# Block 0's left and right sides evicted whole, its context put inside block 1, block 1's rows turned by VectorE

## The chip, the cores and the metric

The kernel runs on one core of a Trainium2 chip. The metric is the time of one execution on the device, in microseconds. A core has five engines that run side by side and wait for one another by semaphores: TensorE (PE; its weight loads are listed as PEld), VectorE (DVE), ScalarE (ACT), GpSimd (POOL) and SyncE (SP), which here only issues DMAs. DMAs are issued from the queues of SyncE, ScalarE and GpSimd. Each engine works through its own instructions in program order, so an instruction that waits holds up all that stand behind it on its engine.

## The reference

Everything is float32. `x` is [128, 64, 768]: 128 graphs of 64 nodes, `adj` is [128, 64, 64]. Two layers, each followed by a residual and a layer norm.

```
layer 0, per graph:
u    = x x^T / sqrt(768);  p = softmax(u);  delta = p * adj
attn = delta / (sum(delta) + 1e-10)
ctx  = upper(attn) (x W_left^T + b_left) + diag(attn) * (x W_self^T + b_self)
       + lower(attn) (x W_right^T + b_right)
x    = layernorm(x + relu(layernorm(ctx) * gamma + beta))
layer 1, per graph, 12 heads of 64:
q, k, v = x Wq + bq, x Wk + bk, x Wv + bv
s    = q k^T / 8 + beta1 * adj, masked where adj <= 0
x    = layernorm(x + softmax(s) v)
```

## The kernel before, in words

The 8192 rows are cut into 16 blocks of 512 rows: four tiles `t` of 128 rows, each holding two graphs (`g`). Layer 0 of block `n+1` is interleaved with layer 1 of block `n`. The last loop (`for n in range(NBLK)`) is that steady part; ahead of it stands a hand-written start, the part that the change edits: layer 0 of block 0, then layer 0 of block 1, while all six weight matrices are turned into the forms that the steady loop reads.

**Products with fewer multiplications.** A product of 512 rows with a 768x768 matrix is done in seven smaller ones (`seven`, `by_tokens`), in the order 1, 2, 6, 5, 7, 4, 3. Each of the seven is done for two halves `j` of the tokens, three matmuls of 128x384 each (the profile counts each float32 matmul as two). The partial sums sit in two PSUM tags, `ps_X` (1, 6, 7, 4) and `ps_Y` (2, 5, 3), with two buffers each. After a group VectorE evicts it: after 1, 6 and 7 into a temporary `u` (line 575, adding a bias), after 2, 7, 4 and 3 into the result (`last`). A group that goes on adding to a bank must wait until the bank's eviction is done, so a late VectorE stops TensorE. A group of 12 takes TensorE 3.87 us. Between groups `step()` takes one waiting piece of other work off a queue (`first`, `urgent`, `lazy`): sums of weights, softmax, norms.

**Weights.** `prepare` loads a matrix in quarters (`b_s`, `b_l`, `b_r`), VectorE forms differences (`t_s`, `t_l`, `t_r`; lines 352 and 354), and the results are stored to DRAM (`d_s`, `d_l`, `d_r`) for block 1. `prepare1` does Wv, Wq and Wk: nine raw pieces are loaded from ScalarE's queue (line 268) into *homes*, VectorE forms fifteen sums, and GpSimd's queue stores them (`v_d`, line 275; `qk_d`, lines 282 and 284). A home is used again when its store has landed. For Wv there are 16 homes (six slices of a transposed-row tile `xT`, four of the later outputs `x1`, six of the pool `prep`), for Wq and Wk 11 of the pool `prep1`, which lies where `prep` was.

**Rows.** A block's rows must be transposed before they can be multiplied. Blocks 0 and 1 are transposed by TensorE (`transposed`, line 397), with ScalarE copying the result out of PSUM (line 398). From block 2 on the rows are loaded in 32x32 order (`squares`, line 407) and VectorE turns them (`turned`, line 416, six instructions of 128x512 per block). The rows of block 1 are loaded by SyncE into `rows` (line 1216).

**Attention and context.** `attention0` runs the scores `u` (line 703), then the softmax, and GpSimd forms the sums of rows (`combined`). `sides` transposes the attention weights (`ps_a`, line 754). `context0` multiplies them with the left and right results, 8 matmuls of 64x384 for two tiles (`ps_ctx`, line 879), and VectorE adds the diagonal part (line 887). Its last part starts the norm: statistics, square root (ScalarE, line 518), scale (910, 914), residual (917), a second norm (924, 928), after which `transposed1(0)` turns block 0 for layer 1.

**The layout that the context needs.** For the context the left result of the second graph has to lie in the upper 64 partitions beside the right result. Block 0 does it in the eviction: two instructions on 64 partitions each (line 807). Blocks 1 and on evict 128 partitions in one (line 801), and ScalarE swaps the two half-tiles later through a spare tile (`swapped`, lines 786 to 788: three copies of 64x768 per tile).

**Order in the start.** Scores of block 0; self of block 0 (weights `b_s`, `t_s`); left of block 0 (`b_l`, `t_l`), while `b_r` is prepared; `sides(0)`; right of block 0, while Wv is prepared; all of block 0's context; rows of block 1 transposed; scores of block 1; then self, left and right of block 1 (`ws`, `wl`, `wr`), while Wq and Wk are prepared; `transposed1(0)`; then the steady loop. The Tile scheduler orders each engine's instructions by the priority of their place in the program and by its estimate of times; `tc.issue_after(x)` forbids a place ahead of `x`. SyncE's queue holds, in order: `xa` (block 0's rows), `b_s`, `bs`, two `adj`, `rows`, `b_l`, the left and right biases, gamma, beta, `bv`, a third `adj`, `b_r`, `bq` and `bk` in columns (line 103), `abeta`, and then `ws`.

Of the kernel before, what the change touches and what calls it, by code (L numbers as in the profile page):

```python
# [17 lines left out]
P = 128  # L18
# [52 lines left out]
def gnn_two_layers(ctx: ExitStack, tc, x, adj, wl, bl, ws, bs, wr, br, gamma, beta,  # L71
# [29 lines left out]
    def column(v, name):  # L101
        t = const.tile([P, KC], F32, tag=name, name=name)
        nc.sync.dma_start(out=t, in_=v.rearrange("(c p) -> p c", p=P))  # L103
        return t
# [6 lines left out]
    abeta_c = const.tile([P, 1], F32, tag="abeta", name="abeta")  # L111

# [123 lines left out]
    def homes_of_v():  # L236

        xT = tp.tile([P, KC, NTOK], F32, tag="xT", name="h_v")
        yield from (xT[:, c, :] for c in range(KC))
        for t in range(T):  # L240
            yield x1_p.tile([P, D], F32, tag="x1", name="h_v")[:, 0 : 2 * TH]

    def prepare1(nm, homes, queue=lazy):
# [16 lines left out]
        def loaded(i):  # L260
# [6 lines left out]
            with tc.issue_after(recent["exp"].ins) if nm == "v" else ExitStack():  # L267
                nc.scalar.dma_start(out=raw, in_=w[:, 2 * k : 2 * k + 2, j * TH : (j + 1) * TH])
# [416 lines left out]
    def attention0(n, sums=True):  # L685
# [13 lines left out]
        for t in range(T):  # L699
            for c in range(KC):  # L700
                for g in range(2):
                    tok = slice(t * P + g * L, t * P + (g + 1) * L)
                    nc.tensor.matmul(u[g * L : (g + 1) * L, t, :], lhsT=xT[:, c, tok], rhs=xT[:, c, tok],  # L703
                                     start=(c == 0), stop=(c == KC - 1))
# [77 lines left out]

    def swapped(lr, t):
# [4 lines left out]
        nc.scalar.copy(low, swap[0:L, 0:D])  # L788

    def side_part(n, nm, in_sbuf, hooks={}):  # L790
# [7 lines left out]
        def last(t, h, ps, part):  # L798
            cols = slice(h * HALF, (h + 1) * HALF)
            if n > 0:  # L800
                recent["u"] = nc.vector.tensor_tensor(lr[t][:, "lr".index(nm), cols], ps,
                                                      bias[nm][:, cols] if part is None else part, ALU.add)
                return
            for g in range(2):
                rows = slice(g * L, (g + 1) * L)
                half = "lr".index(nm)
                recent["u"] = nc.vector.tensor_tensor(lr[t][half * L : (half + 1) * L, g, cols], ps[rows],
                                                       bias[nm][rows, cols] if part is None else part[rows], ALU.add)
# [48 lines left out]
    def context0(n):  # L857
# [13 lines left out]
        banks = {}  # L871
# [10 lines left out]
        def part(t):  # L882
# [8 lines left out]
            elif t == T - 1:  # L891
# [305 lines left out]

    def now(fs):
# [9 lines left out]
    edges(0)  # L1208
    attention0(0)
# [4 lines left out]
    rows = sq_p.tile([P, T, D], F32, tag="sq", name="rows")  # L1214
    for t in range(T):
        nc.sync.dma_start(out=rows[:, t, :], in_=x_t[1, t])
    blocks[1]["rows"] = [rows[:, t, :] for t in range(T)]
# [333 lines left out]
```

## Time and profile before

| | us |
|---|---|
| median of three runs | 2799.73 |
| lowest and highest | 2798.21, 2800.53 |
| the profiled execution | 2799.42 |
| its span | 2797.7 |

The span is the stretch that the trace covers; 1.7 us of the execution lie around it. In the page each group of instructions has its line, engine, operation, output, input, count, busy time, mean duration and the idle time of the engine just before it with what ended it. In a timeline a row is a start, a length, the engine, the line and the operation, and in square brackets the idle time before it. The mean granted TensorE clock of the core is given as 0.999.

### The profile page before, as it was taken

What the parts mean: (1) busy time and instruction counts of PE and PEld (TensorE: products, weight loads), DVE (VectorE), ACT (ScalarE), POOL (GpSimd) and SP (SyncE); (2) the same over time, 40 slices, a digit from 0 to 9 for tenths busy, and PEclk for the clock granted to TensorE, in tenths of its full rate; (3) what the DMA queues carried; (4) which work ended last, traced back from release to release, by engine and by line L of the source; (5) the groups of instructions that cost most, each with busy time, mean ns of one, the idle gap of its engine ahead of it and who ended that gap; (6) DMA issues with size and microseconds to landing.
All of it is one profiled execution on the core that took longest, in us unless ns stands there. A gap on an engine that the chain in (4) does not pass through costs nothing.

```text
span 2797.7 us, 49397 instructions
## 1 busy us (share of the span) xinstructions
PE 2775.1 (99%) x17962; PEld 2013.5 (72%) x17962; DVE 1934.7 (69%) x3380; ACT 1115.1 (40%) x1916; POOL 962.6 (34%) x1251
## 2 busy tenths in 40 slices
PE   8999999999999999999999999999999999999998
PEld 5558677686776867768587685867768677686787
DVE  5767668676675766767677676776767668676667
ACT  0014344335343452434525344353433534345244
POOL 3243334415144141432415225061351513415122
PEclk9999999999999999999999999999999999999999
DMA  9687787958769486695866858578585876948543
GB/s 339 199 299 248 216 256 242 264 151 250 208 186 275 142 267 189 196 266 151 268 180 211 249 170 269 159 229 233 182 259 157 249 208 183 279 143 260 177 129 110
DMA packets 394848, 604.88 MB, mean 216 GB/s; under 512 B 49296, under 2 KB 277648, under 8 KB 394608
## 3 DMA queue, kind: packets, MB, share of 16 engines
q1 hardware_dynamic: 338992, 495.73, 59.3%
q0 software_dynamic: 18704, 76.89, 7.6%
q10 hardware_dynamic: 36912, 29.10, 5.1%
q8 instruction: 146, 2.39, 0.4%
q14 instruction: 94, 0.77, 0.1%
HBM read 530.00 MB, written 78.45 MB: 217 GB/s over the span
## 4 chain that ended last, share of the span: by engine, by line
PE 94%; DVE 2%; DMA 2%; issue 1%; SPq 0%; ACT 0%; POOL 0%; POOLq 0%; DVEq 0%; ACTq 0%
PE ps_X L480 26%; PE ps_Y L480 17%; PE ps_Y L836 13%; PE ps_X L836 11%; PE ps_X L542 10%; PE ps_Y L542 8%; PE ps_ctx L879 3%; PE sc L1041 2%; PE u L703 2%; PE ps_y L1104 2%; PE ps_X L588 1%; DMA qk_d<-h_qk 1%; SPq L103 0%; PE ps_x L397 0%; DMA h_qk<-in_L_gnn_Wk_dram 0%
## 5 line engine op out<-in xcount | busy, mean ns | idle before, releaser
L428 POOL TENSOR_TENSOR sums<-hT 128x768 f32<-128x768 f32 x16 | 29.0, 1811 | 790.3 <-PE ps_X L480 775.5
L1074 ACT ACTIVATE eT<-s 32x384 f32<-32x384 f32 x512 | 266.6, 521 | 33.6 <-PE ps_y L1104 17.0
L480 PE MATMUL ps_X<-xT,wqk 128*128 128x256 f32 x1024 | 234.2, 379 | 0.2 <-ACT xT L398 0.2
L890 ACT ACTIVATE unused<-o 128x768 f32<-128x768 f32 x60 | 50.6, 843 | 440.5 <-DMA sq<-in_x_dram 224.4
L610 DVE TENSOR_TENSOR lr<-ps_Y,u_deep 128x384 f32<-128x384 f32 x273 | 151.7, 556 | 95.3 <-PE ps_Y L836 78.8
L1017 ACT ACTIVATE qk<-ps_X,bq 128x256 f32<-128x256 f32 x128 | 60.7, 474 | 386.9 <-PE ps_X L480 386.6
L480 PEld LDWEIGHTS ps_X<-xT,wqk 128*128 128x128 f32 x1024 | 194.5, 190 | 26.8 <-ACT xT L398 0.4
L836 PE MATMUL ps_Y<-wlr,q 128*128 128x384 f32 x546 | 208.5, 491 | 0.0
L1020 DVE TENSOR_TENSOR qk<-qk,ps_X 128x512 f32<-128x512 f32 x160 | 109.5, 685 | 126.7 <-PE ps_X L480 66.9
L1115 POOL TENSOR_TENSOR o<-o,share 128x192 f32<-128x192 f32 x240 | 135.5, 593 | 148.7 <-DVE share L1112 148.7
L480 PE MATMUL ps_Y<-more,wqk 128*128 128x256 f32 x768 | 181.4, 379 | 0.0
L480 PE MATMUL ps_X<-sums,wqk 128*128 128x256 f32 x768 | 180.8, 382 | 0.6 <-issue 0.3
L458 POOL TENSOR_TENSOR more<-xT 128x512 f32<-128x512 f32 x32 | 40.0, 1272 | 374.9 <-DVE xT L416 184.9
L480 PEld LDWEIGHTS ps_Y<-more,wqk 128*128 128x128 f32 x768 | 145.8, 190 | 19.9
L480 PEld LDWEIGHTS ps_X<-sums,wqk 128*128 128x128 f32 x768 | 144.4, 190 | 21.7 <-DVE qk L1020 1.0
L542 PE MATMUL ps_X<-ws,hT 128*128 128x384 f32 x462 | 154.0, 486 | 0.0
L610 DVE TENSOR_TENSOR u_deep<-ps_X,lr 128x384 f32<-128x384 f32 x195 | 107.6, 552 | 66.8 <-PE ps_X L836 57.5
L1020 DVE TENSOR_TENSOR qk<-qk,ps_Y 128x512 f32<-128x512 f32 x160 | 108.3, 677 | 65.5 <-PE ps_Y L480 63.6
L836 PEld LDWEIGHTS ps_Y<-wlr,q 128*128 128x128 f32 x546 | 101.5, 190 | 67.3 <-DVE lr L610 1.1
L836 PE MATMUL ps_X<-wlr,q 128*128 128x384 f32 x364 | 149.1, 491 | 0.0
L1155 ACT ACTIVATE unused<-o 128x768 f32<-128x768 f32 x56 | 47.3, 844 | 224.9 <-POOL o L1115 222.4
L542 PEld LDWEIGHTS ps_X<-ws,hT 128*128 128x128 f32 x462 | 87.7, 190 | 61.0
(278 smaller groups left out, 6341.8 us busy)
## 6 DMA issues: line engine op xcount, KB each, us to landing
wlr<-lr_d SPq DMA_DIRECT2D x819, 192.0 KB, 3.5
wqk<-qk_d SPq DMA_DIRECT2D x480, 256.0 KB, 2.7
wv<-v_d SPq DMA_DIRECT2D x240, 256.0 KB, 5.8
ws<-d_s SPq DMA_DIRECT2D x180, 192.0 KB, 6.9
ws<-in_L_gnn_W_self_dram SPq DMA_DIRECT2D x135, 192.0 KB, 3.9
xa<-in_x_dram SPq DMA_DIRECT2D x64, 384.0 KB, 5.4
out_dram<-o POOLq DMA_DIRECT2D x60, 384.0 KB, 7.8
sq<-in_x_dram ACTq DMA_DIRECT2D x56, 384.0 KB, 8.8
```

The costliest lines, as they stand in the source:

```text
L480: nc.tensor.matmul(ps[:, h, :], lhsT=a, rhs=b, start=start and h == 0 and k == 0, stop=k == len(fs[h]) - 1, skip_group_check=True)
L542: nc.tensor.matmul(ps, lhsT=a, rhs=b, start=(c == 0 and i in (1, 2, 5)), stop=(c == len(fs) - 1), skip_group_check=True)
L610: nc.vector.tensor_tensor(dst, view(ps), add, ALU.add)
L703: nc.tensor.matmul(u[g * L : (g + 1) * L, t, :], lhsT=xT[:, c, tok], rhs=xT[:, c, tok], start=(c == 0), stop=(c == KC - 1))
L836: nc.tensor.matmul(ps, lhsT=a, rhs=b, start=(k == 0 and j in (1, 2, 5)), stop=(k == len(fs) - 1), skip_group_check=True)
L879: nc.tensor.matmul(ps[g * L : (g + 1) * L, 0:HALF], lhsT=blk["aT"][:, t, g * L : (g + 1) * L], rhs=blk["lr"][t][:, g, h * HALF : (h + 1) * ...
L1017: nc.scalar.activation(dst[:, h], ps[:, h, :], AF.Identity, bias=bias["qk"[h]][:, c : c + 1], scale=float(sign))
L1020: nc.vector.tensor_tensor(dst, dst, ps, ALU.add if sign > 0 else ALU.subtract)
L1041: nc.tensor.matmul(sc[t // 2, r][g * L : (g + 1) * L, t % 2, c, :], lhsT=q[rows, c, tok], rhs=k[rows, c, tok], start=True, stop=True)
L1074: nc.scalar.activation(e[to[0], :, to[1]], pairs[rows, :, cols], AF.Exp, scale=1.0 / SCALE)
L1104: nc.tensor.matmul(y[h, r][cols, t, c, :], lhsT=eT[rows, 2 * h + t, c, cols], rhs=by_parity[rows, 2 * h + t, 2 * c + m, g, :], start=True, ...
L1115: nc.gpsimd.tensor_tensor(res, res, share[:, t], ALU.add)
```

## The change

Six things are changed.

1. A zeroed tile `blank` is multiplied seven times by itself at the very start; the result, `unread`, is not used.
2. Block 1's rows are loaded by `squares` on SyncE's queue, behind `b_l`, and turned by VectorE inside the left side of block 0 (hook 4). The tile they go to is one that held six homes of Wv; so Wv has 12 homes, two of them in a pool `s2` that is idle here, and those in `prep` are taken last.
3. Block 0's left and right results are evicted whole, as in block 1; ScalarE swaps the half-tiles (`swapped_by_halves`, five copies per tile through a narrower spare tile), for tiles 2 and 3 inside the right side, for 0 and 1 after it, all behind the last load of Wv. Block 1 uses the same swap.
4. The scores of block 1 come directly after the right side of block 0. Block 0's context is put into self of block 1: tiles 2 and 3 at its start, 0 and 1 after its third group of matmuls. The norm starts when the last tile is done, whichever it is.
5. The biases `bq` and `bk` are loaded as rows of 128 and transposed by TensorE into one tile `bias_qk` that ScalarE copies out.
6. `prep1` has 16 homes for Wq and Wk. Some loads change place on SyncE's queue: gamma, beta and `bv` now stand behind `b_r`.

```diff
-    def column(v, name):
-        t = const.tile([P, KC], F32, tag=name, name=name)
-        nc.sync.dma_start(out=t, in_=v.rearrange("(c p) -> p c", p=P))
-        return t
+    blank = tmp.tile([P, HALF], F32, tag="u0", name="blank")
+    nc.vector.memset(blank, 0.0)
+    unread = ps_mm.tile([P, 512], F32, tag="mm", name="unread")
+    for _ in range(7):
+        nc.tensor.matmul(unread[:, 0:P], lhsT=blank[:, 0:P], rhs=blank[:, P : 2 * P], start=True, stop=True)
...
+    bias_qk = const.tile([P, 2 * KC], F32, tag="bias_qk", name="bias_qk")
+    bias["q"], bias["k"] = bias_qk[:, 0:KC], bias_qk[:, KC : 2 * KC]
...
     def homes_of_v():
-        xT = tp.tile([P, KC, NTOK], F32, tag="xT", name="h_v")
-        yield from (xT[:, c, :] for c in range(KC))
+        for _ in range(2):
+            yield s2_p.tile([P, 5, P], F32, tag="q", name="h_v").rearrange("p k c -> p (k c)")[:, 0 : 2 * TH]
         for t in range(T):
             yield x1_p.tile([P, D], F32, tag="x1", name="h_v")[:, 0 : 2 * TH]
...
             with tc.issue_after(recent["exp"].ins) if nm == "v" else ExitStack():
-                nc.scalar.dma_start(out=raw, in_=w[:, 2 * k : 2 * k + 2, j * TH : (j + 1) * TH])
+                recent["raw"] = nc.scalar.dma_start(out=raw, in_=w[:, 2 * k : 2 * k + 2, j * TH : (j + 1) * TH])
...
+    swap0 = {}
+
+    def swapped_by_halves(lr, t):
+
+        low, high = lr[t][0:L, 1, :], lr[t][L:P, 0, :]
+        if not swap0:
+            swap0[0] = s2_p.tile([P, 5, P], F32, tag="q", name="swap").rearrange("p k c -> p (k c)")
+        for h in range(2):
+            nc.scalar.copy(swap0[0][h * L : (h + 1) * L, 0:HALF], high[:, h * HALF : (h + 1) * HALF])
+        nc.scalar.copy(high, low)
+        for h in range(2):
+            nc.scalar.copy(low[:, h * HALF : (h + 1) * HALF], swap0[0][h * L : (h + 1) * L, 0:HALF])
...
         def last(t, h, ps, part):
             cols = slice(h * HALF, (h + 1) * HALF)
-            if n > 0:
-                recent["u"] = nc.vector.tensor_tensor(lr[t][:, "lr".index(nm), cols], ps,
-                                                      bias[nm][:, cols] if part is None else part, ALU.add)
-                return
-            for g in range(2):
-                rows = slice(g * L, (g + 1) * L)
-                half = "lr".index(nm)
-                recent["u"] = nc.vector.tensor_tensor(lr[t][half * L : (half + 1) * L, g, cols], ps[rows],
-                                                       bias[nm][rows, cols] if part is None else part[rows], ALU.add)
+            recent["u"] = nc.vector.tensor_tensor(lr[t][:, "lr".index(nm), cols], ps,
+                                                  bias[nm][:, cols] if part is None else part, ALU.add)
...
+    def turn0_of_1():
+        blocks[1]["hT"] = turned(("t", 1), blocks[1]["sq"], "hT_1")
...
     edges(0)
+    rows_qk = tmp.tile([P, T, L], F32, tag="adj", name="rows_qk", bufs=3).rearrange("p t l -> p (t l)")[0 : 2 * KC, 0:P]
+    for k, b in enumerate((bq, bk)):
+        nc.sync.dma_start(out=rows_qk[k * KC : (k + 1) * KC], in_=b.rearrange("(c p) -> c p", p=P))
     attention0(0)
...
     edges(1)
-    rows = sq_p.tile([P, T, D], F32, tag="sq", name="rows")
-    for t in range(T):
-        nc.sync.dma_start(out=rows[:, t, :], in_=x_t[1, t])
-    blocks[1]["rows"] = [rows[:, t, :] for t in range(T)]
     in_sbuf_l = prepare("l", wst, prep, (2, 1, 0))
+    blocks[1]["sq"], load = squares(x_b[1], nc.sync)
+    now(load)
     nc.sync.dma_start(out=bias["l"], in_=bl.partition_broadcast(P))
-    self_part(0, in_sbuf)
+    with tc.issue_after(recent["scores"].ins):
+        self_part(0, in_sbuf)
...
-    side_part(0, "l", in_sbuf_l)
+    side_part(0, "l", in_sbuf_l, {4: [turn0_of_1]})
...
-        homes[0:0] = [(-1, free[:, k * 2 * TH : (k + 1) * 2 * TH]) for k in range(2)]
+        homes += [(-1, free[:, k * 2 * TH : (k + 1) * 2 * TH]) for k in range(2)]
     prepare1("v", homes)
-    side_part(0, "r", in_sbuf_r)
+    swaps = [partial(swapped_by_halves, blocks[0]["lr"], t) for t in range(T)]
+
+    def in_turn(f):
+        with tc.issue_after(recent["raw"].ins):
+            f()
+
+    side_part(0, "r", in_sbuf_r, {12: [partial(in_turn, swaps[2])], 13: [partial(in_turn, swaps[3])]})
+    in_turn(lambda: now(swaps[:2]))
     settle(("w", "v"))
     with tc.issue_after(streamed["b", "r"].ins):
-        bias["q"], bias["k"] = column(bq, "bq"), column(bk, "bk")
         nc.sync.dma_start(out=abeta_c, in_=abeta.partition_broadcast(P))
...
-    prep = streams.enter_context(tc.tile_pool(name="prep1", bufs=11))
-    homes = [(-1, prep.tile([P, 2 * TH], F32, tag="h", name="h_qk")) for _ in range(11)]
-    now(context0(0)[0])
+    prep = streams.enter_context(tc.tile_pool(name="prep1", bufs=16))
+    homes = [(-1, prep.tile([P, 2 * TH], F32, tag="h", name="h_qk")) for _ in range(16)]
+    tiles = context0(0)[0]
+    settle(("t", 1))
     attention0(1)
+    turned_qk = ps_mm.tile([P, 512], F32, tag="mm", name="ps_qk")[:, 0 : 2 * KC]
+    nc.tensor.transpose(turned_qk, rows_qk, ident[0 : 2 * KC, 0 : 2 * KC])
+    nc.scalar.copy(bias_qk, turned_qk)
 
     recent["bound"] = True
-    self_part(1, None, {9: [partial(prepare1, "q", homes, queue=urgent)]})
+    self_part(1, None, {0: tiles[2:3], 1: tiles[3:], 3: tiles[0:1], 4: tiles[1:2], 9: [partial(prepare1, "q", homes, queue=urgent)]})
...
     blocks[2]["sq"], load = squares(x_b[2])
-    now(load)
+    with tc.issue_after(recent["exp"].ins):
+        now(load)
...
             if n == 0:
                 for t in range(T):
-                    at(val, t, swapped, blocks[m]["lr"], t)
+                    at(val, t, swapped_by_halves, blocks[m]["lr"], t)
```

More of the change, by code (lines that the diff above doesn't have):

```diff
@@ L702, in attention0 @@
                     tok = slice(t * P + g * L, t * P + (g + 1) * L)
-                    nc.tensor.matmul(u[g * L : (g + 1) * L, t, :], lhsT=xT[:, c, tok], rhs=xT[:, c, tok],
-                                     start=(c == 0), stop=(c == KC - 1))
+                    recent["scores"] = nc.tensor.matmul(u[g * L : (g + 1) * L, t, :], lhsT=xT[:, c, tok],
+                                                        rhs=xT[:, c, tok], start=(c == 0), stop=(c == KC - 1))
         if sums:
@@ L869, in unused @@
             return l1s_p.tile([P, T * 6 * L], F32, tag="s", name="unused")[:, 0:D]
-        banks = {}
+        banks, open_ = {}, set(range(T))
         def multiplied(ts):
@@ L890, in part @@
                 nc.scalar.activation(unused(), o[t], AF.Identity, accum_out=total[:, t : t + 1])
-            elif t == T - 1:
+            open_.discard(t)
+            if not by_act and not open_:
                 rest(moments(key, o, 1e-12))
```

## The prediction

> **What bounds the kernel now.** I read the engines' busy time first, then the same by stage, then TensorE in order of time where a stage is not full.
>
> ```profile
> PE 2775.1 (99%) x17962; PEld 2013.5 (72%) x17962; DVE 1934.7 (69%) x3380; ACT 1115.1 (40%) x1916; POOL 962.6 (34%) x1251
> ```
>
> ```profile
> 0.00:20.00 20.00, 15.21 (x140) 11.95 (x141) 6.67 (x7) 5.19 (x10) 8.47 (x15) 1.00 0.91 320
> ...
> 40.00:60.00 20.00, 18.58 (x59) 10.71 (x58) 10.98 (x23) 0.00 (x0) 5.51 (x11) 1.00 0.98 330
> ...
> 180.00:200.00 20.00, 18.68 (x73) 12.01 (x72) 13.10 (x30) 7.31 (x13) 9.68 (x13) 1.00 0.68 225
> ...
> 400.00:2700.00 2300.00, 2299.50 (x15007) 1679.39 (x15006) 1596.22 (x2736) 974.89 (x1669) 799.72 (x1038) 1.00 0.72 213
> ```
>
> Columns: window, its length, busy time of PE, PEld, DVE, ACT, POOL, the granted clock, the DMA share, GB/s. TensorE is idle 22.6 us of 2797.7. From 400 to 2700 us it lacks 0.5 us: nothing that the edit does to another engine there can shorten it. All that can be won lies in the first 200 us: TensorE's holes, and TensorE work that can be dropped. The holes, from TensorE's timeline (start, length, group, idle before it and its releaser):
>
> ```profile
> 52.81 2.10 PE L542 MATMUL ps_Y<-t_l,sums 128*128 128x384 f32 x6
> 56.33 2.17 PE L542 MATMUL ps_Y<-t_l,sums 128*128 128x384 f32 x6 [1.42 <-DVE lr L807]
> 58.34 4.03 PE L542 MATMUL ps_X<-b_l,hT 128*128 128x384 f32 x12
> 63.34 4.14 PE L542 MATMUL ps_X<-t_l,hT 128*128 128x384 f32 x12 [0.97 <-DVE u L575]
> ...
> 98.81 3.08 PE L879 MATMUL ps_ctx<-lr,a 128*64 128x384 f32 x16
> 102.40 0.87 PE L879 MATMUL ps_ctx<-lr,a 128*64 128x384 f32 x4 [0.51 <-DVE o L887]
> 103.52 2.16 PE L879 MATMUL ps_ctx<-lr,a 128*64 128x384 f32 x12 [0.26 <-DVE o L887]
> 105.61 3.61 PE L397 MATMUL ps_x<-ident,rows 128*128 128x128 f32 x24
> 109.15 3.02 PE L703 MATMUL u<-hT 128*64 128x64 f32 x96
> 112.10 4.14 PE L542 MATMUL ps_X<-ws,hT 128*128 128x384 f32 x12
> ...
> 181.32 2.20 PE L542 MATMUL ps_Y<-wr,sums 128*128 128x384 f32 x6 [0.79 <-DVE lr L801]
> 184.06 8.06 PE L542 MATMUL ps_X<-wr,hT 128*128 128x384 f32 x24 [0.54 <-DVE u L575]
> ```
>
> A full group of 12 takes 3.87 us from start to start (41.20, 45.08, 48.95), which is the yardstick below.
>
> **1. Seven unread matmuls at the start.** TensorE does nothing before 4.06 us. Between 10.8 and 11.3 us it issues 16 score matmuls in 0.5 us, afterwards 24 to 26: its pace rises at 11.3 us, although the profile's clock column says 1.00 throughout. The Trainium skill (TensorE: Matmul & The Clock Gate, Part 1) says the array starts at half rate and is released after about 3.4 us of sustained work. The pitch of the transposes agrees: 0.21 us here, 0.15 us in the 24 at 105.61. By that rule the warm start is worth 24 x 0.06 us less the waits for `xa`, plus (3.38 - 3.02) us on the scores: about 1.3 us. The row says nothing of it arrives:
>
> ```profile
> 23.68 1.59 PEld L542 LDWEIGHTS ps_X<-t_s,sums 128*128 128x128 f32 x6 [0.69 <-DVE u L575]
> ```
>
> Here TensorE waits for VectorE's eviction, and that chain starts at 13.30 us with a wait of 11.55 us for the DMA of `b_s`, which no edit moves. TensorE would come earlier and wait longer. Bounds: -0.3 us (the seven end after `xa` has landed) to +1.3; I take 0, by the row.
>
> **2. Left side of block 0: whole evictions, and six transposes by VectorE.** Before, an eviction is two instructions of 0.555 us (L807); whole, it is one of 0.556 us (the L801 row, block 1). Eight go on each side, 4.4 us of VectorE each. In their place the left side gets six 32x32-wise transposes of 128x512 at 1.09 us (the L416 row): 6.5 us. So VectorE gets 2.1 us more there, yet the order changes: before, the `t_r` subtraction at 54.47 us sat idle 6.14 us on the DMA of `b_r` with the eviction that TensorE needed queued behind it. In the built program of the changed kernel both Y evictions stand ahead of `t_r`. I add VectorE's queue from the end of `t_l` (43.4): transposes and evictions end at 52.2; three `t_r`, u, three `t_r`, `b_r` (1.35), u, three `t_r`, abeta, add, u end at 59.75, with 0.47 to 0.56 us for each 128x384 operation (back to back they take 0.49). TensorE without holes needs that last u at 52.81 + 2 x 3.87 = 60.6. Full cover would end the left side at 52.81 + 4 x 3.87 = 68.3 instead of 71.19: 2.9 us.
>
> What may spoil it is DMA. Its share is 0.9 to 1.0 until 52 us. The rows of block 1 now come as 2048 pieces of 768 B behind `b_l` instead of 512 of 3 KB ahead of it. For 768 B the skill (DMA: Bandwidth & Descriptors, Specifications) names no loss, since only below 512 B does it say line rate is missed: equal cost. The trace differs: between 106 and 112 us the ScalarE queue moved 1246 packets, 1.11 MB, at 60.8% of 16 engines, 47 ns each, so 2048 take 6.0 us; at 16 to 20 us SyncE's took 108 ns for 2.6 KB, so 512 of 3 KB take 4.1 us. I use 6.0. Three Wv loads more come early (0.75 us each, same 47 ns) and two `v_d` stores; gamma, beta, bv (4.8 us: 36 to 40 us moved 0.95 MB) and an `adj` leave the queue ahead of `b_r`, and the 1536 four-byte pieces of bq and bk go (52 to 56 us shows 1642 packets under 512 B). The old rows landed 7.1 to 8.5 us after issue; issued by 33 us, the new land near 41, and may be as late as 44.2 before TensorE feels it. `b_r` I put near 52. I take 2.5 of the 2.9 us; ends -1 and 2.9.
>
> **3. From right side of block 0 to self of block 1.** Before, 98.81 to 112.10: 13.29 us for 32 context matmuls with holes, 24 transposes (3.54), scores. After: scores 2.95, one small transpose of bias rows (0.15, a transpose's pitch), context 2 x 2.75 (an undisturbed half at 380.18), 0.2 for two extra changes of group: 8.8. Gain 4.5 us, if nothing waits. Now the context needs ScalarE to swap half-tiles first: 64x768 takes 0.83 us (L786); no row shows 64x384, bounds 0.42 (half) and 0.83; I take 0.45, near half, since L398's 128x384 takes 0.48. A tile costs 4 x 0.45 + 0.83 = 2.6 us. Tiles 2 and 3 are fully evicted near 90.7 and 92.7, so swapped at 92.8 and 95.4, before scores end at 99.4; tiles 0 and 1 at 98 and 102, needed near 107. Covered; if the cover goes, 2.6 us for each tile. Queued on ScalarE behind them: the h_qk loads, the bias copy and the exponential. The fourth bank of the first half waits for that copy, itself behind an h_qk issue waiting for the last `v_d` stores: 0 to 1 us, I take 0.1. Gain 4.4.
>
> **4. Block 0's normalization, 16 homes for Wq and Wk.** At 175.5 to 180.7 us VectorE stood still for a square root that ScalarE (idle 54.89 us) held behind Wk loads waiting for `qk_d` stores. TensorE started at 184.06 what a full pace gives at 178.44 + 3.87 = 182.31: 1.75 us lost. With 16 buffers these loads reuse only long-stored ones, and the root stands later in VectorE's order. I take 1.5; ends 0 and 1.75. The price of the later context: block 0's scale factors come with the X7/X4 evictions, near 181 us; four ScalarE normalizations of 0.96 us end near 185, and the transposes that read them start near 187. Two us of cover where there were eight. ScalarE then does three half copies and a 64x768 of block 1's swap just ahead of the xT copies: -0.4 us, ends -1.5 and 0. SyncE's queue is passed by nothing urgent: `xa` of block 1 waits for block 0's residual, with later weights behind it, but `wr` is loaded over 20 us before use (143.36 against 166.82).
>
> **Sum.** 0 + 2.5 + 4.4 + 1.5 - 0.4 = 8.0 us off the profiled execution's 2799.42 (span 2797.7 and 1.7 around it): 2791.4; the median of the three runs is 0.3 higher, so **2791.8 us**. After 200 us the same full TensorE runs, earlier.
>
> **Rivals.**
> - *Late bytes on the left side* (16%): `b_r` or the rows land 3 us later than I put them; part 2 gives -0.5 instead of 2.5, the rest stays: 2794.8. For it: DMA is full there. Against: 5 us of slow broadcast leaves the queue.
> - *ScalarE's queue replaces the old holes* (12%): the root or the normalizations are late by 3 us at 187, so part 4 gives -1.9: 2794.8. For it: ScalarE runs in order and now has h_qk issues between swaps. Against: two us of cover.
> - *VectorE blocked by the first transpose* (8%, slower): it stands ahead of the first left eviction and waits for all four row loads. VectorE has 16.4 us of work from there to the u that TensorE needs at 60.6, so each us past 44.2 is lost whole; past 44.2 + 8.0 = 52.2 us the change loses. If the rows land as late as `b_r` did (54.5) plus the 3.5 us of their heavier neighbours, at 58: 2805.6. Against: the 7.7 us landing of the old rows.
>
> **Numbers.** The forecast has 64% (2789.8 to 2794). The range, 2789.8 to 2796.8, takes in the first two rivals and the low ends of parts 2 to 4. A measurement can tell about 0.2% (5.6 us) from none, so faster means below 2794.1: the forecast and some of the milder rivals, 70%; no change 22%; slower 8%.
>
> **What would show it.** Right: no TensorE hole over 0.3 us between 52 and 70; scores directly after `b_r`'s last group; contexts without a wait on ScalarE; no hole near 175 to 180; `u` at 23.7 still awaited with transposes done sooner. Wrong: VectorE idle at its first transpose on the `sq` DMA, or at `t_r`; TensorE waiting on `lr` or `bias_qk` from ScalarE; ps_x of block 0 waiting on `o`; any new hole past 200 us.

## The result, and the profile after

| | median us | lowest to highest | profiled execution | its span |
|---|---|---|---|---|
| before | 2799.11 (16 runs) | 2797.16 to 2802.83 | 2799.42 | 2797.7 |
| after | 2805.01 (16 runs) | 2802.96 to 2807.40 | 2805.17 | 2803.4 |

The ratio is 1.0021, with a 95% interval of 1.0014 to 1.0027. The change costs 5.9 us; the prediction had it win 8. In the line numbers of the changed kernel the matmul of layer 0 is L545 (before L542), the evictions are L578 and L816 (L575 and L801), the context is L888, the sums of rows on GpSimd are L461 (L458), the sums of weights L304 and L306.

First the engines' busy time and the same stages as before (window, its length, busy time of PE, PEld, DVE, ACT and POOL, granted clock, DMA share, GB/s):

```profile
PE 2777.9 (99%) x17953; PEld 2014.7 (72%) x17953; DVE 1931.6 (69%) x3371; ACT 1123.4 (40%) x1937; POOL 963.1 (34%) x1251
```

```profile
40.00:60.00 20.00, 18.08 (x56) 10.09 (x54) 14.99 (x24) 0.00 (x0) 5.20 (x10) 1.00 1.04 387
...
140.00:160.00 20.00, 17.63 (x52) 9.99 (x51) 14.16 (x24) 0.51 (x1) 8.06 (x12) 0.94 1.00 340
160.00:180.00 20.00, 20.00 (x64) 11.78 (x64) 18.18 (x41) 0.71 (x2) 7.07 (x11) 0.98 0.88 321
180.00:200.00 20.00, 20.00 (x81) 13.90 (x80) 9.47 (x23) 11.03 (x20) 6.10 (x9) 1.00 0.58 196
200.00:220.00 20.00, 14.65 (x57) 10.45 (x56) 6.90 (x11) 7.55 (x14) 13.81 (x13) 0.83 0.54 173
...
400.00:2700.00 2300.00, 2299.58 (x14947) 1678.85 (x14949) 1594.65 (x2735) 973.60 (x1666) 794.17 (x1033) 1.00 0.73 213
```

The steady part is as full as it was, and 180 to 200 us, which lacked 1.32 us before, is now full. Two other stages now lack TensorE time: 2.4 us between 140 and 160 (none before) and 5.4 us between 200 and 220 (0.2 before). There, and just behind the first, the granted clock is below 1.00; before it was 1.00 in all of them. TensorE's timeline (start, length, group, idle before it and its releaser):

```profile
57.34 2.20 PE L545 MATMUL ps_X<-b_l,hT 128*128 128x384 f32 x6 [1.46 <-DVE u L578]
60.48 2.20 PE L545 MATMUL ps_X<-b_l,hT 128*128 128x384 f32 x6 [0.94 <-DVE u L578]
...
98.27 3.02 PE L706 MATMUL u<-hT 128*64 128x64 f32 x96
101.21 0.23 PE L1268 MATMUL ps_qk<-ident,rows_qk 12*128 12x12 f32 x1
101.37 1.51 PE L888 MATMUL ps_ctx<-lr,a 128*64 128x384 f32 x8
103.15 1.51 PE L888 MATMUL ps_ctx<-lr,a 128*64 128x384 f32 x8 [0.27 <-ACT bias_qk L1269]
104.59 4.14 PE L545 MATMUL ps_X<-ws,hT 128*128 128x384 f32 x12
...
156.60 5.83 PE L545 MATMUL ps_X<-wl,hT 128*128 128x384 f32 x12 [2.37 <-DVE u L578]
162.27 4.03 PE L545 MATMUL ps_Y<-wl,sums 128*128 128x384 f32 x12
...
182.06 7.90 PE L545 MATMUL ps_X<-wr,hT 128*128 128x384 f32 x24
193.67 3.54 PE L400 MATMUL ps_x<-ident,o 128*128 128x128 f32 x24
...
206.03 6.74 PE L483 MATMUL ps_X<-wv,sums 128*128 128x256 f32 x16 [5.35 <-POOL sums L461]
```

Comparing the starts of equal groups in both traces gives an account of where the lead was won and lost:

| group | before | after | lead of after |
|---|---|---|---|
| left side of block 0, first group | 41.20 | 40.23 | 0.97 |
| the same, last group | 67.32 | 66.77 | 0.55 |
| left side of block 1, first group | 139.30 | 134.72 | 4.58 |
| the same, last group | 162.52 | 162.27 | 0.25 |
| transposes of block 0 for layer 1 | 195.83 | 193.67 | 2.16 |
| first group of layer 1 that reads sums of rows | 202.51 | 206.03 | -3.52 |
| scores of block 2 | 237.39 | 242.72 | -5.33 |

So the context and the scores bring what was forecast, and it is lost in two holes that were not there before. Each costs more than its idle time: the 12 matmuls behind the **first hole** take 5.83 us instead of 4.03, the 16 behind the **second** 6.74 instead of 3.62. The latter in the kernel before:

```profile
202.51 3.62 PE L480 MATMUL ps_X<-wv,sums 128*128 128x256 f32 x16
```

What released them? For the first hole, ScalarE's timeline (ACTq lines are DMA issues) and VectorE's:

```profile
141.37 0.51 ACT L801 COPY swap<-lr 64x384 f32<-64x384 f32 x1 [17.25 <-DVE lr L816]
147.33 0.38 ACTq L271 DMA_DIRECT2D h_qk<-in_L_gnn_Wk_dram  x1
147.75 0.55 ACTq L271 DMA_DIRECT2D h_qk<-in_L_gnn_Wq_dram  x1
```

```profile
154.52 0.69 DVE L306 TENSOR_TENSOR h_qk<-h_qk 128x512 f32<-128x512 f32 x1 [5.11 <-DMA h_qk<-in_L_gnn_Wq_dram]
155.13 0.95 DVE L927 SCALAR_TENSOR_TENSOR o<-o,xa 128x768 f32<-128x768 f32 x1
156.00 0.55 DVE L578 TENSOR_TENSOR u<-ps_X,bias_lr 128x384 f32<-128x384 f32 x1
```

Read backwards: TensorE waits for the eviction at 156.00, which stands on VectorE behind a sum of Wq at 154.52, which waited 5.11 us for a piece of Wq that was issued only at 147.75. On ScalarE's queue two things stand ahead of it: a copy of block 1's swap, which the scheduler has pulled into the left side (141.37), and the first load of Wk (147.33). For the second hole, GpSimd's timeline, after and before, and VectorE's, after:

```profile
201.40 2.49 POOL L461 TENSOR_TENSOR more<-xT 128x512 f32<-128x512 f32 x2 [5.28 <-DMA w_deep<-d_l]
```

```profile
198.31 2.51 POOL L458 TENSOR_TENSOR more<-xT 128x512 f32<-128x512 f32 x2
```

```profile
201.09 0.69 DVE L1000 TENSOR_TENSOR v<-bv,ps_X 128x512 f32<-128x512 f32 x1 [6.00 <-DMA qk_d<-h_qk]
```

Before, `more` started at 198.31, while ScalarE's copies of `xT` still ran (196.41 to 199.73), directly behind the issue of the last store of `qk_d` in GpSimd's own queue. Now that store is issued at 195.39 and the copies end near 197.9, yet `more` waits until 201.40 for a DMA. The transfer named reads a weight that `more` doesn't use. VectorE's row shows another that lands just then: an eviction into `v` had to wait until 201.09 for a store of `qk_d`. The pool of `more` is made after the pool of the homes is closed and takes its memory; with five more homes, the space of 16 reaches to where `more` lies. If so, it waits for the last stores of `qk_d`.

### The profile page after: what moved, and what is told of

Same layout as the page of the kernel before. It is cut to its first block, busy times and chain, and to the rows that moved or that the text cites. A ratio compares the mean times of both kernels' runs of the same rounds, so it can differ in the third digit from the quotient of the medians.

```text
span 2803.4 us, 49378 instructions
## 1 busy us (share of the span) xinstructions
PE 2777.9 (99%) x17953; PEld 2014.7 (72%) x17953; DVE 1931.6 (69%) x3371; ACT 1123.4 (40%) x1937; POOL 963.1 (34%) x1251
## 4 chain that ended last, share of the span: by engine, by line
PE 95%; DMA 2%; DVE 2%; issue 1%; POOL 0%; SPq 0%; ACT 0%; ACTq 0%; DVEq 0%; POOLq 0%
PE ps_X L483 26%; PE ps_Y L483 17%; PE ps_Y L845 13%; PE ps_X L845 11%; PE ps_X L545 10%; PE ps_Y L545 8%; PE ps_ctx L888 3%; PE sc L1051 2%; PE ps_y L1114 2%; PE u L706 2%; PE ps_X L591 1%; DMA b_r<-in_L_gnn_W_right_dram 1%; DMA h_qk<-in_L_gnn_Wq_dram 0%; DMA b_s<-in_L_gnn_W_self_dram 0%; PE ps_a L757 0%
## 5 line engine op out<-in xcount | busy, mean ns | idle before, releaser
L1027 ACT ACTIVATE qk<-ps_X,bias_qk 128x256 f32<-128x256 f32 x256 | 107.5, 471 | 387.0 <-PE ps_X L483 386.8
L461 POOL TENSOR_TENSOR more<-xT 128x512 f32<-128x512 f32 x32 | 40.0, 1270 | 381.5 <-DVE xT L419 183.6
L545 PE MATMUL ps_X<-ws,hT 128*128 128x384 f32 x462 | 154.0, 486 | 0.0
L545 PEld LDWEIGHTS ps_X<-ws,hT 128*128 128x128 f32 x462 | 87.7, 190 | 61.5 <-DMA h_qk<-in_L_gnn_Wq_dram 0.6
```

Of the source, the lines that this page charges most:

```text
L545: nc.tensor.matmul(ps, lhsT=a, rhs=b, start=(c == 0 and i in (1, 2, 5)), stop=(c == len(fs) - 1), skip_group_check=True)
L1027: nc.scalar.activation(dst[:, h], ps[:, h, :], AF.Identity, bias=bias["qk"[h]][:, c : c + 1], scale=float(sign))
```

## The experiments

The theory for the first hole was that Wk's first load, waiting for a store of `qk_d` to land, held Wq's last load (rivals: the swap copy; bytes). For the second it was memory (rival: the sums of Wk are late by themselves). Each time is a median, beside the runs of the kernel before on the same chip.

**The loads of Wk behind those of Wq.**

```diff
-    side_part(1, "l", None, {9: [partial(prepare1, "k", homes, queue=urgent)]})
+    side_part(1, "l", None, {11: [partial(prepare1, "k", homes, queue=urgent)]})
```

> The changed kernel, with the sums of Wk begun two hooks later (11 for 9 in the left side of block 1), so that the last load of Wq stands ahead of the first load of Wk on ScalarE's queue. Theory 'order of the loads': TensorE's hole of 2.37 us at 156.60 comes from the last Wq load, issued at 147.75, behind a Wk load that waited until 147.33 for a store of qk_d to land. Then the Wq load goes out near 142, VectorE's idle 5.11 us ahead of the sum at 154.52 goes, the group at 156.60 has no hole over 0.5 us and the next ones run at 3.9 us, and block 1's next ps_Y starts near 158.5 instead of 162.27. Rival 'the swap': ScalarE's half copy at 141.37 is what is in the way; then the hole stays over 1.5 us. Rival 'bytes' (DMA share 1.00 between 140 and 160): the piece lands as late and the hole stays. The hole of 5.35 us at 206.03 stays by all three (more lead is lost in it), so the time is the changed kernel's, within 2 us.

Measured: 2801.21 us (before 2799.01; ratio 1.0008, 0.9999 to 1.0017). TensorE's timeline:

```profile
150.03 7.90 PE L545 MATMUL ps_X<-wl,hT 128*128 128x384 f32 x24
157.77 4.03 PE L545 MATMUL ps_Y<-wl,sums 128*128 128x384 f32 x12
...
201.32 5.14 PE L483 MATMUL ps_X<-wv,sums 128*128 128x256 f32 x16 [5.14 <-POOL sums L461]
```

The 24 matmuls run through without a hole; the last group of the left side starts 4.50 us earlier than in the changed kernel, with the same bytes to move, so bytes were not the cause. Wq's last piece goes out at 143.01 although the swap copy still stands ahead of it, at 141.21. One part of the expectation missed: the lead is not given back in the second hole, which only moves 4.7 us forward, because the stores it waits for move with the rest. The time fell by 3.8 us.

**The swap of block 1 as before.**

```diff
-                    at(val, t, swapped_by_halves, blocks[m]["lr"], t)
+                    at(val, t, swapped, blocks[m]["lr"], t)
```

> The changed kernel with block 1's swap done as before (three copies of 64x768 through a tile that exists only in the steady loop), so no swap copy can stand among the Wq and Wk loads on ScalarE. Theory 'the swap': the hole of 2.37 us at 156.60 goes and block 1 is about 4 us earlier at 162. Theory 'order of the loads': the first Wk load still waits for its store until about 147 with the last Wq load behind it, and the hole stays between 1.5 and 2.8 us. The hole at 206.03 stays by both, perhaps 0.5 to 1 us less because the xT copies have no half copies ahead of them.

Measured: 2805.84 us (before 2799.01; ratio 1.0025, 1.0016 to 1.0034). TensorE's timeline:

```profile
157.51 2.20 PE L545 MATMUL ps_X<-wl,hT 128*128 128x384 f32 x6 [1.36 <-DVE u L578]
160.10 2.20 PE L545 MATMUL ps_X<-wl,hT 128*128 128x384 f32 x6 [0.39 <-DVE u L578]
```

The hole stays, in two pieces of 1.36 and 0.39 us, and the last left group starts at 162.14 (162.27). It is shorter than in the changed kernel, but TensorE also came to the left side 1.9 us later in this execution (136.63 for 134.72). Without the copy ScalarE stood at the Wk load until 148.54, and Wq's last piece followed at 148.97. The swap is not the cause. Here the group behind the hole was not slowed.

**Eleven homes, and sixteen in the kernel before.**

```diff
-    prep = streams.enter_context(tc.tile_pool(name="prep1", bufs=16))
-    homes = [(-1, prep.tile([P, 2 * TH], F32, tag="h", name="h_qk")) for _ in range(16)]
+    prep = streams.enter_context(tc.tile_pool(name="prep1", bufs=11))
+    homes = [(-1, prep.tile([P, 2 * TH], F32, tag="h", name="h_qk")) for _ in range(11)]
```

The second kernel is the one before with this edit the other way round.

> The changed kernel with 11 homes for Wq and Wk, as before, instead of 16. Theory 'memory': the 5.35 us hole at 206.03 comes from GpSimd's first sum of rows (more), whose memory lies where the five added homes were, and so waits for the last stores of qk_d. Then more starts right after the xT copies (near 196 to 198), the hole is under 1 us, the group of 16 behind it takes 3.6 us instead of 6.74, and about 8 us are won there; a hole of 0.5 to 2 us may come back near 175 to 184, where VectorE waits for the square root. Expected 2797 to 2800. Rival 'late sums': the Wk sums are late because of the loads, not because of memory; then the hole stays over 3 us and the time within 2 us of the changed kernel's 2805.

> The kernel before with 16 homes for Wq and Wk instead of 11, nothing else. Theory 'memory': more must wait for the last store of qk_d here too; a hole of 2 to 6 us appears ahead of the first group of block 0's layer 1 that reads sums (202.51 before), the group behind it slows from 3.62 to 5 to 7 us, the holes at 181.32 and 184.06 go, and the kernel is 2 to 8 us slower than before. Rival 'late sums': no hole there; the kernel is 1 to 2 us faster than before, as the prediction had it for part 4.

Measured: the changed kernel with 11 homes takes 2798.41 us (ratio 0.9998, 0.9990 to 1.0007), the kernel before with 16 takes 2805.24 (1.0021, 1.0013 to 1.0028; before 2799.01). TensorE and GpSimd in the kernel before with 16 homes, at the lines of that kernel:

```profile
181.14 7.90 PE L542 MATMUL ps_X<-wr,hT 128*128 128x384 f32 x24
...
192.75 3.38 PE L397 MATMUL ps_x<-ident,o 128*128 128x128 f32 x24
...
204.94 6.56 PE L480 MATMUL ps_X<-wv,sums 128*128 128x256 f32 x16 [5.35 <-POOL sums L458]
```

```profile
200.33 2.48 POOL L458 TENSOR_TENSOR more<-xT 128x512 f32<-128x512 f32 x2 [5.12 <-DMA w_deep<-d_l]
```

This one number, 11 to 16, makes the second hole at its full length in a kernel in which nothing else was changed, and the whole loss of 6 us with it. It also does what it was to do: the holes of 0.79 and 0.54 us at 181 and 184 are gone, and the transposes start 3.1 us earlier than before. With 11 homes in the changed kernel both new holes are gone (the loads of Wq and Wk get other homes, and their order on ScalarE is another), but one of 2.05 us is left. TensorE's and GpSimd's timeline there:

```profile
199.45 3.72 PE L483 MATMUL ps_X<-wv,sums 128*128 128x256 f32 x16 [2.05 <-POOL sums L461]
```

```profile
193.21 2.49 POOL L461 TENSOR_TENSOR more<-xT 128x512 f32<-128x512 f32 x2 [0.60 <-ACT xT L401]
198.01 0.18 POOL L1297 MEMSET v<- 128x48 f32 x1 [2.31 <-DMA qk_d<-h_qk]
198.13 2.50 POOL L461 TENSOR_TENSOR sums<-xT,more 128x512 f32<-128x512 f32 x2
```

`more` starts right behind the `xT` copies. Then a fill of 0.18 us, the columns of ones in `v`, waits for the same store and holds the sums behind it. Before it stood behind all of them.

**The ones behind the sums, on 11 homes.** Here `recent["rows_sum"]` is the last instruction of `fifteen`.

```diff
-    recent["ones"] = nc.gpsimd.memset(v[:, :, :, HD], 1.0)
+    with tc.issue_after(recent["rows_sum"].ins):
+        recent["ones"] = nc.gpsimd.memset(v[:, :, :, HD], 1.0)
```

> The changed kernel with 11 homes, and with the fill of v's columns of ones placed behind GpSimd's sums of rows, as it stood before. With 11 homes alone the fill (0.18 us at 198.01) waited 2.31 us for the last store of qk_d with the sums behind it. Theory 'queue of GpSimd': the sums start at 195.7, the group of 16 that reads them at about 197.2 instead of 199.45, its 2.05 us hole goes, and the kernel takes about 2 us less than with 11 homes alone (2798.4): 2795 to 2797. Rival 'PSUM': VectorE's evictions into v, which wait for the same store until 197.75, hold the banks that the group needs; then less than 0.7 us is won.

Measured: 2795.51 us (before 2799.01; ratio 0.9986, 0.9980 to 0.9993).

```profile
199.48 3.62 PE L483 MATMUL ps_X<-wv,sums 128*128 128x256 f32 x16
```

The group that reads the sums has no hole before it. It started at 199.48, not 197.2, since this execution's TensorE was 2.2 us later at the transposes (192.40 against 190.16); from transposes to group it took 7.08 us instead of 9.29. That is the first version to beat both kernels.

**Is the time behind a hole the array's own?** The changed kernel, with work in its second hole:

```diff
+                def fill():
+                    idle = ps_mm.tile([P, 512], F32, tag="mm", name="idle")
+                    for _ in range(28):
+                        nc.tensor.matmul(idle[:, 0:P], lhsT=ident, rhs=ident, start=True, stop=True)
+
+                at(val, 2, fill)
```

> The changed kernel (16 homes) with 28 unread matmuls of 128x128 put into its hole of 5.35 us, directly ahead of the group of 16 at 206.03. Theory 'cold array': the group takes 6.74 us instead of 3.62 because TensorE stood still before it; with 28 x 0.15 = 4.2 us of work in the hole it takes 3.6 to 4.2 us and the kernel is 2.5 to 3.1 us faster than the changed one (2805). Rival 'operands late': the matmuls of the group wait for the sums one by one; then the group still takes over 6 us and the time stays.

Measured: 2803.51 us (before 2799.01; ratio 1.0017, 1.0010 to 1.0024), 1.5 us under the changed kernel by the medians, less than the 2.5 to 3.1 expected, and 3.3 by the spans of the profiled executions (2800.1, 2803.4). The intervals of the two ratios overlap, so the trace has to decide.

```profile
199.93 6.41 PE L1414 MATMUL idle<-ident 128*128 128x128 f32 x56
206.18 3.62 PE L483 MATMUL ps_X<-wv,sums 128*128 128x256 f32 x16
```

The group starts at the same time and takes 3.62 us instead of 6.74. So its operands were there, and the 3.1 us are the price of having stood still. (The first hole was not filled; its 1.8 us rest on the granted clock.) The fill was longer than I had put it, 0.23 us a matmul (6.41 / 28) instead of 0.15, and covered the hole whole.

**The start and the left side of block 0.** On the run with 11 homes and the ones later, three edits, each alone: no unread matmuls; gamma, beta and `bv` loaded later; rows of block 1 in larger pieces. The third leaves these rows in another order, so block 1 is computed from wrong rows and columns; only its times are of use.

```diff
-    unread = ps_mm.tile([P, 512], F32, tag="mm", name="unread")
-    for _ in range(7):
-        nc.tensor.matmul(unread[:, 0:P], lhsT=blank[:, 0:P], rhs=blank[:, P : 2 * P], start=True, stop=True)
```

```diff
-    affine_of["gamma"] = row(gamma, "gamma")
...
+        with tc.issue_after(recent["u"].ins):
+            nc.vector.memset(d[nm][:, 0:1], 0.0)
+        nc.sync.dma_start(out=d[nm], in_=v_.partition_broadcast(P))
```

```diff
-    blocks[1]["sq"], load = squares(x_b[1], nc.sync)
-    now(load)
+    blocks[1]["sq"] = sq_p.tile([P, SQ, Q * KC], F32, tag="sq", name="sq")
+    for a in range(P // Q):
+        nc.sync.dma_start(out=blocks[1]["sq"][a * Q : (a + 1) * Q].rearrange("p s f -> p (s f)").rearrange("p (t d) -> p t d", t=T),
+                          in_=x_t[1].rearrange("t p d -> p t d")[a * Q : (a + 1) * Q])
```

> The run with 11 homes and the ones later, without the seven unread matmuls. The changed kernel was 0.97 us ahead at its first left group (40.23 against 41.20). Theory 'it is the warm start': that lead goes; transposes and scores slow again (24 in more than 4.7 us, scores 3.4), the first left group starts near 41.2, and all after it stands about 1 us later, the end included. Rival 'it is the order of the loads in the start' (b_s is issued by 4.7 us instead of 5.7, rows of block 1 no longer ahead of b_l): the lead stays over 0.6 us without the warm start.

> The run with 11 homes and the ones later, with gamma, beta and bv loaded behind the left side of block 0 (each waits for a 128x1 fill by VectorE that stands there), so their bytes are not under way while b_r lands. Theory 'bytes': b_r lands 3 us earlier than in the changed kernel (VectorE's t_r at 52.3 instead of 55.32), the holes of 1.46 and 0.94 us at 57.34 and 60.48 go, the group at 66.77 starts at 64.4, and the kernel is 2 to 2.4 us faster than the same one without this edit. Rival 'pieces of 768 bytes': block 1's rows, ahead of b_r in the queue, are what delays it; then b_r comes less than 1 us earlier and less than 1 us is won.

> The run with 11 homes and the ones later, with block 1's rows loaded at the same place of SyncE's queue, the same 1.5 MB, but as 512 pieces of 3 KB instead of 2048 of 768 B (block 1 is then computed from rows and columns in another order). Theory 'pieces of 768 bytes': they are what makes b_r late. Then b_r lands 2 to 4 us earlier (VectorE's first t_r at 51.5 to 53.3 instead of 55.3), the holes of 1 to 1.5 and 0.94 us at 57 and 60 go or fall below 0.3 us, and the first right group starts near 68.5 instead of 70.9. Rival 'all bytes': the queues are full whatever the pieces; b_r moves by less than 1 us and the holes stay.

Measured: without the warm start 2796.66 us (ratio to the kernel before 0.9993, 0.9985 to 1.0001), with gamma, beta and `bv` later 2796.43 (0.9993, 0.9985 to 1.0001), with pieces of 3 KB 2795.21 (0.9988, 0.9982 to 0.9995). Without these edits it was 0.9986, inside or beside each of the intervals, so the reading rests on the traces. Without the warm start:

```profile
10.41 4.07 PE L701 MATMUL u<-hT 128*64 128x64 f32 x96
...
60.30 2.20 PE L540 MATMUL ps_X<-b_l,hT 128*128 128x384 f32 x6 [0.94 <-DVE u L573]
```

The scores take 4.07 us instead of 3.02, and the left side begins at 41.60 instead of 40.45. Sixteen us later nothing is left of it: the group that waited 1.04 us for VectorE at 57.13 starts at 57.16 without a wait. The warm start did what it says, and its 1.15 us went into the next wait.

With gamma, beta and `bv` out of the way `b_r` came no earlier: VectorE's first difference `t_r` started at 56.50 (55.11 without the edit, 55.32 in the changed kernel). With pieces of 3 KB it started at 54.60. Neither the 1.2 MB behind `b_r` nor the pieces of 768 bytes ahead of it explain more than 0.7 us. All these runs have one slow stretch: from 34 to 40 us, just as `b_r` is issued, the full queues move 199 GB/s in the changed kernel, 201 and 207 in these two, and 368 to 387 in the 6 us that follow. What makes it slow, and so sets the landing of `b_r` some 15 us after its issue, stays open.

**The bias early, then all repairs.** The two blocks of code for the bias and the homes:

```diff
+    turned_qk = ps_mm.tile([P, 512], F32, tag="mm", name="ps_qk")[:, 0 : 2 * KC]
+    nc.tensor.transpose(turned_qk, rows_qk, ident[0 : 2 * KC, 0 : 2 * KC])
+    nc.scalar.copy(bias_qk, turned_qk)
     side_part(0, "l", in_sbuf_l, {4: [turn0_of_1]})
```

```diff
-            home = min(homes, key=lambda h: h[0])
+            free = [h for h in homes if nm != "k" or done[0] <= 8 or not any(h[1] is e for e in extra)]
+            home = min(free, key=lambda h: h[0])
...
-    prep = streams.enter_context(tc.tile_pool(name="prep1", bufs=16))
+    prep = streams.enter_context(tc.tile_pool(name="prep1", bufs=11))
+    above = streams.enter_context(tc.tile_pool(name="prep2", bufs=5))
+    extra = [above.tile([P, 2 * TH], F32, tag="h2", name="h_qk") for _ in range(5)]
```

> The run with 11 homes and the ones later, with the bias rows turned and copied ahead of the left side of block 0, where ScalarE is idle, instead of between the scores and the context. There TensorE waited 1.36 us (104.34) for ScalarE's copy of 0.17 us, queued behind a Wq load that waited for the last store of Wv. Theory 'queue of ScalarE': the wait goes and self of block 1 begins about 1.3 us earlier behind the scores (X group 3.2 us after the context begins instead of 4.3). At the end 0 to 1.3 us less than 2795.5, since the last stores of qk_d must come earlier too. Rival 'the swap is what is late' (the third swapped half-tile ends at 104.8): the wait stays over 0.8 us, with another releaser.

> All repairs at once: 16 homes of which the five that lie under the sums of rows are given to Wk only for its first sums, Wk's loads behind Wq's, the ones later, the bias early. Theory: no hole over 0.5 us at 156 (order of the loads), none at 175 to 185 (16 homes), and more starts right behind the xT copies (memory), so TensorE is contiguous from 106 to 199 and the kernel takes 2793 to 2795.5. Rival 'the last store decides': v's memory still waits for the last store of qk_d, and TensorE's lead is given back in a hole of 1 to 2.5 us between 195 and 207; then 2795 to 2797.

Measured: 2795.49 us with the bias early (before 2798.68; ratio 0.9988, 0.9981 to 0.9994), against 2795.51: the wait of 1.36 us goes and self of block 1 begins 2.69 us behind the context's start, but a hole of 2.17 us opens at 178.74, behind VectorE, and takes the lead. With all repairs (this, the split homes, Wk's loads behind Wq's, the ones later) it is 2792.62 us (ratio 0.9979, 0.9970 to 0.9987). TensorE and GpSimd:

```profile
176.92 7.90 PE L546 MATMUL ps_X<-wr,hT 128*128 128x384 f32 x24
...
195.40 3.64 PE L484 MATMUL ps_X<-wv,sums 128*128 128x256 f32 x16
```

```profile
191.35 2.50 POOL L462 TENSOR_TENSOR more<-xT 128x512 f32<-128x512 f32 x2 [0.37 <-ACT xT L402]
```

From 62 to 199 us TensorE has no hole over 0.3 us. There are still 16 homes; what has changed is which of them lies under `more` and who uses it last. VectorE's eviction into `v` still waits for the last store of `qk_d`, until 196.29; `more` no longer does. The memory theory holds.

**The differences of `b_r` behind the evictions.** On the run with all repairs:

```diff
-            with tc.issue_after(recent["u"].ins) if nm == "l" else ExitStack():
+            with tc.issue_after(recent["u"].ins) if nm in ("l", "r") else ExitStack():
                 subtracted(out, left, right)
```

> The run with all repairs, with the differences of b_r (t_r) held behind VectorE's evictions of the left side of block 0. Theory 'order on VectorE': TensorE's holes near 57 and 60 (0.33 and 0.94 us here, 1.46 and 0.94 in the changed kernel) do not come from the landing of b_r as such but from evictions queued behind t_r, which waits for it; with t_r behind them the holes go, the group at 66.76 starts at 64.6 +- 0.3, and the right side starts near 69 instead of 71.06. At the end 0.8 to 2 us less than 2792.6, so 2790.6 to 2791.8, if the lead is kept. Rival 'the lead is given back': the swaps on ScalarE or the last store of qk_d come no earlier, a hole of 1 to 2 us appears between 90 and 110 or near 200, and the time stays at 2792 to 2793.

Measured: 2791.92 us (before 2798.30; ratio 0.9978, 0.9969 to 0.9986), the lowest median of all.

```profile
55.93 4.03 PE L546 MATMUL ps_X<-b_l,hT 128*128 128x384 f32 x12
61.55 4.14 PE L546 MATMUL ps_X<-t_l,hT 128*128 128x384 f32 x12 [1.59 <-DVE u L579]
65.53 4.03 PE L546 MATMUL ps_Y<-b_l,sums 128*128 128x384 f32 x12
```

The holes at 57 and 60 are gone, so it was the order on VectorE that carried the landing of `b_r` to TensorE. But the next instruction in that queue took most of the gain: a scaling of `abeta` at 60.49 waited 7.67 us for its DMA, with an eviction behind it. From its first group to its last the left side took 25.18 us (40.35 to 65.53) instead of 25.51 (41.25 to 66.76); the rest of the 1.23 us is an earlier start in this execution. That lead is kept to the end of the start (194.17 against 195.40), but the medians, 0.7 us apart, don't tell the two versions from one another.

## Why the prediction was wrong, step by step

- **Step 4, the 16 homes, is the step that failed.** At the scores of block 2 forecast and trace are 13.3 us apart (a lead of 8.0 against -5.33): 11.0 lie in step 4 (a lead of 4.58 became -5.33, where I had 1.1 to win), 2.9 in step 2, 0.4 in step 3, less 1.0 that step 1 won. "With 16 buffers these loads reuse only long-stored ones", I wrote, with ends of 0 and 1.75. Its gain came, a little above my upper end: in the kernel before with 16 homes, the lead over the kernel before grows from 1.17 us (161.35 for 162.52) to 3.08 (192.75 for 195.83), so 1.9. What I left out was the memory: I asked who uses a home next among the loads, and not what lies there once the pool is closed. That cost 5.35 us of hole and 3.1 us of slow matmuls. The sentence was also wrong as it stands: the first Wk load went out only at 147.33, which is when a store of `qk_d` issued at 140.93 lands if it takes the 6.4 us that these stores take in the median (the trace does not name what the load waited for), and on ScalarE's queue the last Wq load stood behind it. That is the first hole, 2.37 us and 1.8 us of slow matmuls.
- **The price of a hole.** All my bounds took a hole as its idle time. The two that came were 7.7 us of idle time (2.37 + 5.35) and cost 4.9 us more (1.80 + 3.12) in the groups behind them.
- **Step 2, the left side of block 0,** was mis-sized by one term, "`b_r` I put near 52": it landed for `t_r` at 55.32, and the step gave -0.4 us (a lead of 0.97 became 0.55) instead of 2.5. That is the first rival, which had -0.5. The evictions and transposes took what was forecast. VectorE in the changed kernel, where the eviction that TensorE needed stood behind `t_r`:

```profile
55.32 1.49 DVE L355 TENSOR_TENSOR t_r<-b_r 128x384 f32<-128x384 f32 x3 [4.32 <-DMA b_r<-in_L_gnn_W_right_dram]
56.73 0.55 DVE L578 TENSOR_TENSOR u<-ps_X,bias_lr 128x384 f32<-128x384 f32 x1
```

- **Step 3, scores and context,** held: 4.0 us (0.55 to 4.58) of the 4.4, with a wait of 0.27 us for the bias where I had put 0.1. It is not always so short: in five of the runs above the same wait was 1.35 to 1.45 us, beyond my end of 1. A copy of 64x384 took 0.51 us, not 0.45, between its bounds.
- **Step 1, the warm start,** held at 0 as far as the end is concerned. The lead of 0.97 us did reach the left side, past the wait at 23 us that I had thought would take it (22.71, still 0.65 us), and was lost at 57.
- **The rivals.** The one on ScalarE's queue named the right queue and the h_qk loads in it, but at 187 us and at 3 us; the transposes of block 0 had no wait there. No rival had an instruction that waits, past 195 us, for memory that a store still reads. Of the signs of being wrong, "any new hole past 200 us" came, and VectorE idle at `t_r`. The slow rival's 2805.6 us lies beside the measured 2805.0 by chance: its cause, rows that land late, did not come, since VectorE's first transpose started at 42.54 without a wait.
- **A reading.** VectorE stood still from 176.1 us, not from 175.5: the row at 175.46 is a sum of 0.68 us. Nothing hangs on it.

With the repairs that the experiments point to, the kernel comes to 2792.6 and 2791.9 us. That the prediction had 2791.8 is partly chance: step 2 still brings little there (0.6 and 0.9 us of 2.5), and steps 3 and 4 more than I took.

## What to carry to other kernels

A pool that grows is paid for where its memory is used next: before adding buffers, see which tiles lie there after it closes, which engine touches them first, and whether the last transfer out of the pool has landed by then. When a wait is taken off a queue, look for the next instruction in it that waits for a transfer, since evictions behind it inherit the wait; twice here the lead went straight into the neighbour. A TensorE hole of some 2 us or more may be followed by slow matmuls: price them too.

## What was not expected of the hardware

TensorE's slowness after a hole came sooner than I knew. The Trainium skill (TensorE: Matmul & The Clock Gate, Part 1) gives an idle window of about 3.4 us before the array falls to half rate. Here 12 matmuls took 5.83 us instead of 4.03 behind a hole of 2.37 us, with a granted clock of 0.94 in that stretch, and 16 took 6.74 instead of 3.62 behind 5.35 us (0.83). Shorter holes did it too: 12 took 5.97 us behind 2.02 (gamma, beta and `bv` later) and 5.83 behind 1.86 (the first hole in the run with the filled second), 24 took 9.70 instead of 7.90 behind 2.17 (bias early). Yet one of 2.05, with 11 homes, left its group of 16 at 3.72. So the length of the hole alone does not decide.

The same columns over short windows show more; the first three rows are the changed kernel around its first hole, the last two the run with 11 homes around the hole of 2.05 us:

```profile
154.14:157.56 3.42, 1.05 (x4) 0.68 (x4) 3.01 (x5) 0.00 (x0) 1.78 (x3) 1.00 0.91 293
157.56:160.97 3.41, 3.41 (x6) 1.64 (x5) 3.38 (x7) 0.00 (x0) 3.41 (x6) 0.50 0.89 281
160.97:164.38 3.41, 3.41 (x12) 2.08 (x11) 3.33 (x6) 0.00 (x0) 1.32 (x2) 1.00 1.04 396
...
195.39:198.81 3.42, 2.01 (x10) 1.43 (x8) 1.06 (x2) 3.31 (x6) 1.11 (x3) 1.00 1.04 397
198.81:202.22 3.41, 2.77 (x13) 2.46 (x14) 1.51 (x3) 3.27 (x7) 3.41 (x4) 1.00 0.93 333
```

In the changed kernel the clock goes to one half at 157.56, a microsecond after the hole has ended, and stays there for 3.41 us; behind the second hole it does so from 205.34 to 212.17, for 6.83 us. In each of the kept traces all changes of the clock lie whole multiples of 3.41 us apart (14 from 157.56 to 205.34), so time is cut into fixed stretches. A fall came whenever TensorE had been idle for 1.86 us or more of the stretch that ended there, and never at 1.72 us or less. The hole of 2.05 us lay across two stretches (1.41 and 0.64 us; their boundary at 198.81 lies 758 of them ahead of that trace's fall at 2786.11) and cost no more than itself. So about half a stretch decides here, and the same hole is slow or not by where it falls; that it is this share that counts is read from the traces, and no run moved a hole on purpose. The clock column shows these falls, though it showed none for the slow matmuls of the first microseconds.

The releaser that the profile names can be a bystander: for the second hole it named a load of a deep weight, where the runs show the last store out of the homes.
